# Row sums of causal attention over added pairs of exponentials: GpSimd adds, TensorE takes four steps in three groups

## The chip, the cores and the metric

The kernel runs on one core of a Trainium2 chip. The metric is the device time of one execution in microseconds (us), as the median of several runs. The core has five engines that work beside each other, each through its own queue in order: TensorE (PE, matrix products), VectorE (DVE), ScalarE (ACT), GpSimd (POOL) and SyncE (SP, which issues the transfers). PE writes its results to PSUM, eight banks of 128 x 512 float32; ACT and DVE read PSUM, POOL does not in this kernel.

## The reference, cut to what matters

One transformer block over 2048 tokens of width 512: a normalization, causal attention with 16 heads of 32, and a gated feed-forward part of width 4096, both added to the input. The change touches the attention alone:

```python
scores = jnp.einsum('bhqd,bhkd->bhqk', q, k) * scale
scores = jnp.where(causal, scores, jnp.finfo(scores.dtype).min)
probs = jax.nn.softmax(scores, axis=-1)
attn = jnp.einsum('bhqk,bhkd->bhqd', probs, v)
```

The softmax is not divided out before the product: the kernel sums `exp(score - max) * v` and `exp(score - max)` over the keys, and divides the one by the other at the end.

## The kernel before, in words

The work has four stages. Up to about 190 us tokens are normalized and transposed, values are made, and the queries, keys and row maxima of the first heads. From there to about 735 us runs the **main attention loop**, over six of the eight head pairs; then to about 848 us the **joint stage**, in which the last two pairs share each step; then the feed-forward part, which the change does not touch.

A head pair p has 40 steps, n = 0 to 39. A step is a block of 512 queries (qb) against a tile of 128 keys (kt). The query blocks come in the order 1, 2, 3, 0 with 8, 12, 16 and 4 steps: n = 0 to 7, 8 to 19, 20 to 35, 36 to 39. The last four steps of each block are on the diagonal, where only the last 512, 384, 256 and 128 columns are computed. They are the **diagonal** steps; all others are full.

The order on PE is written out by hand: the scheduler is off, and each engine gets its instructions in the order of the program. One step of the main loop (L508 to L533) issues, in this order:

- the transposes of finished maxima, if due (`rows_when_due`, L271), four steps after they were split up;
- `score_cols` (L290): for both heads, the product that puts minus the row maximum into a tile of the pool `ps_t`;
- `score_rows` (L216): scores with the queries in the partitions, for a later head pair, into two tiles of the pool `ps_s`. They serve only to find the row maxima;
- `add_scores` (L305): scores with the keys in the partitions, added to the `ps_t` tiles;
- `attend` (L358) for the step two before this one: a **group** of four products of 32 columns each, which lie side by side in the array's four column tiles: values of head 0, values of head 1, and for both heads a matrix of ones, which gives the row sums. All four go to one bank, `av`;
- `exponentials` on ACT (L319; on the diagonal L325, L327 and L329 and then `omit_later_keys`, L334, on POOL);
- `maxima` on DVE (L240, on the diagonal L235), and when a block's maxima are complete, `split` (L250 on DVE, L256 and L258 on POOL);
- `keep_attention`, if a query block was finished one step ago: ACT copies the values out of `av` (L378), DVE the sums (L379);
- `normalize_attention` (L391 on DVE, L393 on POOL), one quarter of a block per full step, after the second pair of each two;
- in some steps a projection of queries or keys for later heads (`project`, L172, eight passes, copied out by L184 or L186 on ACT).

PSUM is full: `ps_s` and `ps_t` have three banks each, and `ps_m` has two (m0 and m1). A step takes two tiles of `ps_s` and two of `ps_t`. The accumulators `av` take m0 and m1 in turn from one query block to the next, and the other one of the two is "spare": projections and transposed maxima use it. The exponentials of a step lie in one of four `prob` tiles.

Of the kernel before, what the change touches and what calls it, by code (L numbers as in the profile page):

```python
# [33 lines left out]
BF16 = mybir.dt.bfloat16  # L37
F32 = mybir.dt.float32
# [3 lines left out]
ALU = mybir.AluOpType  # L42
# [3 lines left out]
P = 128  # L46
# [3 lines left out]
D = H // HEADS  # L50
NT = S // P
TB = 512
NTB = S // TB
NK = H // P
NOG = H // P
NP = HEADS // 2
# [21 lines left out]
def block_kernel(  # L78
# [10 lines left out]
    nc = tc.nc  # L89
# [4 lines left out]
    def turn_tile(i, name, dtype=F32, shape=(P, TB)):  # L94
        return turns.tile(list(shape), dtype, tag=f"turn{i}", name=name)
# [17 lines left out]
    with (  # L113
# [24 lines left out]
        ones = const.tile([P, D], F32, tag="ones", name="ones")  # L138
        nc.vector.memset(ones, 1.0)

        turn = [0]
# [17 lines left out]

        qT, kT = {}, {}

        def project(og, b, which):
            for _ in project_halves(og, b, which):
                pass

        def project_halves(og, b, which):
            w = wqk[og]
            ps = spare(F32, f"ps_qk{og}_{b}_{which}")  # L170
# [21 lines left out]
        units, steps, first = [], [], {}  # L192
# [12 lines left out]
        def tile_of(pool, name):  # L205
            return pool.tile([P, TB], F32, tag="s" if pool is ps_s else "t", name=name)
# [52 lines left out]

            due.append((tick[0] + 4, p, qb, buf))  # L260

        def rows_from_parts(joint):

            _, p, qb, buf = due.pop(0)
            og, half = p // 2, slice(64 * (p % 2), 64 * (p % 2 + 1))
            if p < 2 or joint:
                pt = ps_t.tile([P, TB], BF16, tag="t", name=f"pm{p}_{qb}")
            else:
                pt = spare(BF16, f"pm{p}_{qb}")
# [6 lines left out]
        def rows_when_due(joint=False):  # L276
            if due and tick[0] >= due[0][0]:
                rows_from_parts(joint)
            tick[0] += 1

        def score_cols(p, n, pool):
# [59 lines left out]
                channel_multiplier=-1,  # L341
            )

        avs, sums = {}, {}

        def attend(p, n, prob, first=None, last=None):

            qb, kt = steps[n]
            if first is None:
                first, last = kt == 0, kt == 4 * qb + 3  # L350
            if first:
                turn[0] = (NTB * p + qb) % 2 if p < NP - 2 else p % 2
                avs[p, qb] = ps_m.tile([P, TB], F32, tag=f"m{turn[0]}", name=f"av{p}_{qb}")
            av = avs[p, qb]
            c0 = max(0, kt - 4 * qb) * P
            for h in range(4):
                head = 2 * p + h % 2
                nc.tensor.matmul(  # L358
                    av[D * h : D * (h + 1), c0:],
                    lhsT=v[kt // 4][:, kt % 4, D * head : D * (head + 1)] if h < 2 else ones,  # L360
                    rhs=prob[:, h % 2, c0:],
                    start=first,
                    stop=last,
                )
            if last:
                full.append((p, qb))

        full, invert = [], []

        def keep_attention():  # L370

            p, qb = full.pop(0)
            av = avs[p, qb]
            og, half = p // 2, slice(64 * (p % 2), 64 * (p % 2 + 1))
            if p % 2 == 0:
                sums[og, qb] = sump.tile([P, TB], F32, tag="sums", name=f"sums{og}_{qb}")
            if p < NP - 2:
                nc.scalar.copy(aT[og][qb][half], av[:64])  # L378
                nc.vector.tensor_copy(sums[og, qb][half], av[64:])  # L379
            else:  # L380
# [100 lines left out]
        for b in range(NTB):  # L481
            n = first[b]
# [24 lines left out]
        pending, waiting = [], False  # L507
        for m in range((NP - 2) * STEPS):  # L508
            p, n = divmod(m, STEPS)

            ahead = p + 3 if p % 2 == 0 else p + 1
# [12 lines left out]
            pending.append((p, n, prob))  # L524
            qb, kt = steps[n]
            if invert and kt < 4 * qb:
                normalize_attention()


            if own in places and og + 2 < NOG:  # L530
                project(og + 2, *places[own])
            if own in places_own and og > 0 and og + 1 < NOG:
                project(og + 1, *places_own[own])  # L533
# [40 lines left out]
        def token_rest(b, k, high):  # L574
# [8 lines left out]
            )  # L583
            yield

        early = [(i, k) for i in range(2) for k in range(NK)]
        rest = iter(())
        for s, n in enumerate(together):
            rows_when_due(joint=True)
# [3 lines left out]
            for _ in range(2):  # L593
# [405 lines left out]
```

## Time and profile before

| | us |
|---|---|
| median of 3 runs | 1992.45 |
| lowest, highest | 1990.56, 1992.8 |
| the profiled execution | 1993.41 |
| its span | 1991.7 |

| stretch of the profiled execution, us | length | PE busy | DVE busy | ACT busy | POOL busy |
|---|---|---|---|---|---|
| 205 to 735 (main loop) | 530 | 527.1 | 324.9 | 295.3 | 79.7 |
| 735 to 850 (joint stage) | 115 | 107.8 | 47.1 | 74.6 | 33.9 |
| 1000 to 1990 (feed-forward) | 990 | 985.9 | 712.6 | 604.4 | 521.5 |

The profile is of one execution. Its page gives the busy time of each engine, the span in 40 slices, the chain of work that ended last, and groups of instructions by line with count, mean duration in ns, and the idle time before them with what ended it. The timeline lists instructions in order of time: start, duration, engine, line, operation, what is written and read, the shape, the count, and in brackets the idle time ahead of it and its releaser. A stretch of the windows view has its length, busy time and count of PE, of PE's weight loads (PEld), DVE, ACT and POOL, then the granted clock of PE (1.00 is full), the share of the DMA engines and GB/s. A float32 product takes two passes, so a group of four products shows as eight.

### The profile page before, as it was taken

The page shows a single profiled execution, that of the slowest core. Times are in us where ns is not written, and L with a number is a line of the kernel's source. Part 1 is how long each engine was busy: PE and PEld are TensorE (multiplying, and loading weights), DVE is VectorE, ACT ScalarE, POOL GpSimd, SP SyncE. Part 2 cuts the span into 40 slices and gives each one's busy share as a digit, 9 for nine tenths or more (in the row PEclk, how much of TensorE's full clock was granted, in tenths as well). Part 3 has the DMA queues.
Part 4 walks back from the last instruction along what each step waited for, and adds up shares of the span by engine and source line. Part 5 has one row for each costly group of instructions (what it writes and reads, how often), then busy time and mean ns, then how long its engine had stood idle before and what let it go on. Part 6 is the DMA issues. An engine that isn't in the chain of part 4 may idle for free.

```text
span 1991.7 us, 31028 instructions
## 1 busy us (share of the span) xinstructions
PE 1958.1 (98%) x11072; PEld 1163.9 (58%) x11072; DVE 1326.4 (67%) x2706; ACT 1092.6 (55%) x2281; POOL 727.3 (37%) x893
## 2 busy tenths in 40 slices
PE   7999999999999999999999999999999999999998
PEld 3433233333333323246888888888888888888886
DVE  5657665646565665277777777777777777767674
ACT  2111664546455666634666666666666666666654
POOL 1000111201120224145555555555555555545451
PEclk9999999999999999999999999999999999999999
DMA  3000000000000000120000000000000000000002
GB/s 127 0 11 12 1 2 1 2 12 1 1 1 12 1 1 2 36 73 23 22 20 21 20 21 21 21 20 21 21 20 22 18 23 18 23 18 22 19 5 85
DMA packets 55387, 39.79 MB, mean 20 GB/s; under 512 B 14784, under 2 KB 47552, under 8 KB 55232
## 3 DMA queue, kind: packets, MB, share of 16 engines
q1 hardware_dynamic: 55232, 37.81, 6.4%
q8 instruction: 87, 1.43, 0.3%
q14 instruction: 68, 0.56, 0.1%
HBM read 33.55 MB, written 4.19 MB: 19 GB/s over the span
## 4 chain that ended last, share of the span: by engine, by line
PE 96%; ACT 2%; DVE 1%; issue 1%; DMA 0%; POOL 0%; DVEq 0%; SPq 0%; ACTq 0%; POOLq 0%
PE gu L851 24%; PE av L358 12%; PE gu L864 12%; PE pd L914 12%; PE ps_s L216 9%; PE ps_qk L172 6%; PE pd L926 6%; PE ps_t L290 4%; PE ps_t L305 3%; PE ps_v L462 3%; PE po L806 3%; ACT prob L319 1%; PE pm L271 1%; PE ptx L451 0%; ACT prob L566 0%
## 5 line engine op out<-in xcount | busy, mean ns | idle before, releaser
L851 PE MATMUL gu<-xh,gu 128*128 128x512 f32 x1024 | 404.3, 395 | 0.0
L851 PE MATMUL gu<-lm,gu 128*128 128x512 f32 x1024 | 404.2, 395 | 0.0
L240 DVE TENSOR_REDUCE tops<-ps_s 128x1 f32<-128x512 f32 x384 | 243.7, 682 | 159.0 <-PE ps_s L216 138.2
L935 DVE SCALAR_TENSOR_TENSOR acc<-pd,acc 128x512 f32<-128x512 f32 x512 | 317.0, 681 | 2.4 <-PE pd L926 2.4
L319 ACT ACTIVATE prob<-ps_t 128x512 f32<-128x512 f32 x384 | 205.9, 597 | 158.1 <-PE ps_t L305 156.7
L216 PE MATMUL ps_s<-qk,qk 32*128 32x512 f32 (+3 forms) x1280 | 292.0, 577 | 0.0
L358 PE MATMUL av<-prob,v 128*32 128x512 f32 (+3 forms) x1280 | 288.6, 540 | 2.0 <-issue 0.7
L358 PE MATMUL av<-prob,ones 128*32 128x512 f32 (+3 forms) x1280 | 288.5, 541 | 0.0
L864 PE MATMUL gu<-lm,gu 128*128 128x512 f32 x1024 | 279.8, 395 | 0.0
L896 POOL TENSOR_TENSOR parts<-inter,hi 128x512 fp32r<-128x512 f32 x128 | 171.2, 1338 | 278.2 <-DVE hi L892 273.0
L888 DVE SCALAR_TENSOR_TENSOR inter<-gu,gate 128x512 f32<-128x512 f32 x128 | 88.5, 691 | 275.3 <-PE gu L864 271.0
L305 PE MATMUL ps_t<-qk,qk 32*128 32x512 f32 (+3 forms) x1280 | 265.5, 537 | 0.0
L921 ACT ACTIVATE pd<-pd 128x512 f32<-128x512 f32 x512 | 263.4, 582 | 1.1 <-PE pd L914 1.1
L914 PE MATMUL pd<-wd,parts 128*128 128x512 f32 x1024 | 259.6, 396 | 0.0
L858 ACT ACTIVATE gu<-gu 128x512 f32<-128x512 f32 x256 | 148.7, 581 | 188.2 <-PE gu L851 188.1
L864 PEld LDWEIGHTS gu<-lm,gu 128*128 128x128 f32 x1024 | 192.3, 188 | 46.8 <-issue 0.2
L851 PEld LDWEIGHTS gu<-lm,gu 128*128 128x128 f32 x1024 | 192.2, 188 | 46.1 <-POOL wd L721 0.2
L914 PEld LDWEIGHTS pd<-wd,parts 128*128 128x128 f32 x1024 | 192.4, 188 | 45.6
L851 PEld LDWEIGHTS gu<-xh,gu 128*128 128x128 f32 x1024 | 192.2, 188 | 45.7 <-ACT wd L720 0.2
L334 POOL TENSOR_SCALAR_AFFINE_SELECT prob<-prob 128x256 f32<-128x256 f32 x128 | 52.2, 409 | 424.2 <-ACT prob L329 317.4
L235 DVE CUSTOM_DVE_ANT_0 ps_s<-ps_s,mask_qk 128x128 f32<-128x128 f32 (+3 forms) x256 | 120.8, 516 | 101.3 <-PE ps_t L305 55.7
L895 ACT CAST parts<-hi 128x512 fp32r<-128x512 f32 x128 | 79.7, 623 | 173.1 <-DVE hi L892 173.1
(98 smaller groups left out, 2672.1 us busy)
## 6 DMA issues: line engine op xcount, KB each, us to landing
pk<-packed SPq DMA_DIRECT2D x96, 128.0 KB, 2.2
sc<-scales SPq DMA_DIRECT2D x512, 8.0 KB, 1.6
x<-x SPq DMA_DIRECT2D x16, 256.0 KB, 3.9
acc<-x SPq DMA_DIRECT2D x16, 256.0 KB, 3.7
sc<-scales SPq DMA_DIRECT2D x256, 16.0 KB, 1.7
out<-acc SPq DMA_DIRECT2D x16, 256.0 KB, 2.2
wqk<-w_qk SPq DMA_DIRECT2D x4, 512.0 KB, 3.7
wv<-w_v SPq DMA_DIRECT2D x4, 256.0 KB, 6.5
```

Of the source, the lines that this page charges most:

```text
L216: nc.tensor.matmul(ps[:, :w], lhsT=qT[p // 2, qb][rows, i * P : (i + 1) * P], rhs=kT[p // 2, c][rows, :w], start=True, stop=True,)
L240: nc.vector.tensor_reduce(top, ps[:, :w], AX.X, ALU.max)
L305: nc.tensor.matmul(ps[:, c0:], lhsT=kT[p // 2, kt // 4][rows, (kt % 4) * P : (kt % 4 + 1) * P], rhs=qT[p // 2, qb][rows, c0:], start=False ...
L319: nc.scalar.activation(prob[:, h, :], ps, AF.Exp)
L358: nc.tensor.matmul(av[D * h : D * (h + 1), c0:], lhsT=v[kt // 4][:, kt % 4, D * head : D * (head + 1)] if h < 2 else ones, rhs=prob[:, h % ...
L851: nc.tensor.matmul(ps, lhsT=parts[:, i, k], rhs=mov, start=(k == 0 and i == 0), stop=(k == NK - 1 and i == 1),)
L858: nc.scalar.activation(ps, ps, AF.Copy, scale=HIGH_SCALE)
L864: nc.tensor.matmul(ps, lhsT=gu[g, m, j][:, 2, k], rhs=lm[b, k][1], start=False, stop=(k == NK - 1), skip_group_check=True,)
L896: nc.gpsimd.tensor_tensor(parts[:, 1], inter, high, ALU.subtract)
L914: nc.tensor.matmul(po, lhsT=parts[:, part, i * P : (i + 1) * P], rhs=w[:, part], start=(part == 0), stop=(part == 1),)
L921: nc.scalar.activation(po, po, AF.Copy, scale=HIGH_SCALE)
L935: nc.vector.scalar_tensor_tensor(acc[t], po, SUM_SCALE, acc[t], ALU.mult, ALU.add)
```

## The change

In the full steps of the main loop, the row sums are no longer taken for each step. POOL adds the exponentials of two neighbouring steps (two additions of 128 x 512, one for each head), and PE multiplies the added tile by the matrix of ones. Four full steps then need eight products with values and four with ones, which are put into three groups in place of four:

- `attend_pair`: the values of steps 0 and 1, each with both heads, in all four column tiles of `av`. Column tiles 2 and 3 of `av` so collect part of the values;
- `attend_with_rows`, twice: the values of step 2 (then 3) in column tiles 0 and 1 of `av`, and the ones over an added pair in column tiles 2 and 3 of another bank, `rows`.

The diagonal steps keep a group of their own, with values to `av` and sums to `rows`. `av` is now always m0 and `rows` always m1 in the main loop. So nothing is spare there: the projections take a tile of `ps_s`, the transposed maxima a tile of `ps_t`. `keep_attention` copies values and sums on ACT, and DVE adds the second half of the values (for query block 0, which has only diagonal steps, this is left out). It comes in the step in which the block's last group is issued, no longer one step later. The joint stage keeps groups of four products in one bank.

When a group is issued is set by `later_on`. The built order has, relative to the first step of four: the pair in step 3, the first group with sums in step 4, the second in step 6; a diagonal step's group comes three steps later, that of the last diagonal step two. So of a head pair's 40 steps, n = 2, 5, 10, 13, 17, 22, 25, 29, 33 and 38 issue no group, and n = 1, 9, 21 and 37 issue two (256 and 128 columns). Before, each step issued one.

The diff, cut to its core:

```diff
-        def spare(dtype, name):
-            i = (turn[0] + 1) % 2
-            return ps_m.tile([P, TB], dtype, tag=f"m{i}", name=name)
...
+        def add_values(p, n, prob, place, start, stop):
             qb, kt = steps[n]
             c0 = max(0, kt - 4 * qb) * P
-            for h in range(4):
-                head = 2 * p + h % 2
+            for h in range(2):
+                head = 2 * p + h
+                j = 2 * place + h
                 nc.tensor.matmul(
-                    av[D * h : D * (h + 1), c0:],
-                    lhsT=v[kt // 4][:, kt % 4, D * head : D * (head + 1)] if h < 2 else ones,
-                    rhs=prob[:, h % 2, c0:],
-                    start=first,
-                    stop=last,
-                )
+                    avs[p, qb][D * j : D * (j + 1), c0:],
+                    lhsT=v[kt // 4][:, kt % 4, D * head : D * (head + 1)],
+                    rhs=prob[:, h, c0:],
+                    start=start,
+                    stop=stop,
+                )
+
+        def add_rows(p, qb, probs, c0, start, stop):
+            for h in range(2):
+                nc.tensor.matmul(
+                    rows[p, qb][D * (2 + h) : D * (3 + h), c0:],
+                    lhsT=ones,
+                    rhs=probs[h][:, c0:],
+                    start=start,
+                    stop=stop,
+                )
+
+        def open_sums(p, qb):
+            avs[p, qb] = ps_m.tile([P, TB], F32, tag="m0", name=f"av{p}_{qb}")
+            rows[p, qb] = ps_m.tile([P, TB], F32, tag="m1", name=f"rows{p}_{qb}")
+
+        def attend_pair(p, n, prob_a, prob_b):
+            qb, kt = steps[n]
+            if kt == 0:
+                open_sums(p, qb)
+            add_values(p, n, prob_a, 0, kt == 0, False)
+            add_values(p, n + 1, prob_b, 1, kt == 0, kt == 4 * qb - 4)
+
+        def attend_with_rows(p, n, prob, added, start):
+            add_values(p, n, prob, 0, False, False)
+            add_rows(p, steps[n][0], added, 0, start, False)
...
+        def add_up(q, prob_a, prob_b):
+            added = []
+            for h in range(2):
+                t = turn_tile(2 * (q % 4) + h, f"added{q}_{h}")
+                nc.gpsimd.tensor_tensor(t, prob_a[:, h], prob_b[:, h], ALU.add)
+                added.append(t)
+            return added
...
-            if p < NP - 2:
-                nc.scalar.copy(aT[og][qb][half], av[:64])
-                nc.vector.tensor_copy(sums[og, qb][half], av[64:])
-            else:
-                copy = nc.scalar.copy if p % 2 == 0 else nc.vector.tensor_copy
-                copy(aT[og][qb][half], av[:64])
-                copy(sums[og, qb][half], av[64:])
+            copies = [nc.scalar.copy] * 2
+            if p == NP - 1:
+                copies = [nc.vector.tensor_copy] * 2
+            copies[0](aT[og][qb][half], av[:64])
+            if p < NP - 2 and qb > 0:
+                nc.vector.tensor_tensor(aT[og][qb][half], aT[og][qb][half], av[64:], ALU.add)
+            copies[1](sums[og, qb][half], row[64:])
...
-            if len(pending) == 2:
-                attend(*pending.pop(0))
+            run_due(m)
             prob = exponentials(p, n, ps)
             maxima(ahead, n, ps_max)
-            if waiting:
+            while full:
                 keep_attention()
-            waiting = bool(full)
-            pending.append((p, n, prob))
             qb, kt = steps[n]
+            if kt >= 4 * qb:
+                later_on(2 if kt == 4 * qb + 3 else 3, attend_diagonal, p, n, prob)
+            elif kt % 2 == 0:
+                even = prob
+            else:
+                added = add_up(2 * quads + kt % 4 // 2, even, prob)
+                if kt % 4 == 1:
+                    later_on(2, attend_pair, p, n - 1, even, prob)
+                    added_first = added
+                else:
+                    later_on(1, attend_with_rows, p, n - 1, even, added_first, kt == 3)
+                    later_on(3, attend_with_rows, p, n, prob, added, False)
+                    quads += 1
             if invert and kt < 4 * qb:
                 normalize_attention()
             if own in places and og + 2 < NOG:
-                project(og + 2, *places[own])
+                b, which = places[own]
+                project(og + 2, b, which, tile_of(ps_s, f"ps_qk{og + 2}_{b}_{which}"))
```

More of the change, by code (lines that the diff above doesn't have):

```diff
@@ L139, in block_kernel @@
         nc.vector.memset(ones, 1.0)
-        turn = [0]
-        def spare(dtype, name):
-            i = (turn[0] + 1) % 2
-            return ps_m.tile([P, TB], dtype, tag=f"m{i}", name=name)
         v = [vals.tile([P, 4, H], F32, tag=f"v{b}", name=f"v{b}") for b in range(NTB)]
@@ L162, in block_kernel, with project, project_halves @@
         qT, kT = {}, {}
-        def project(og, b, which):
-            for _ in project_halves(og, b, which):
+        def project(og, b, which, ps=None):
+            for _ in project_halves(og, b, which, ps):
                 pass
-        def project_halves(og, b, which):
+        def project_halves(og, b, which, ps=None):
             w = wqk[og]
-            ps = spare(F32, f"ps_qk{og}_{b}_{which}")
+            if ps is None:
+                ps = ps_m.tile([P, TB], F32, tag="m1", name=f"ps_qk{og}_{b}_{which}")
             for k in range(NK):
@@ L260, in split, with rows_from_parts @@
             due.append((tick[0] + 4, p, qb, buf))
-        def rows_from_parts(joint):
+        def rows_from_parts():
             _, p, qb, buf = due.pop(0)
             og, half = p // 2, slice(64 * (p % 2), 64 * (p % 2 + 1))
-            if p < 2 or joint:
-                pt = ps_t.tile([P, TB], BF16, tag="t", name=f"pm{p}_{qb}")
-            else:
-                pt = spare(BF16, f"pm{p}_{qb}")
+            pt = ps_t.tile([P, TB], BF16, tag="t", name=f"pm{p}_{qb}")
             for i in range(4):
@@ L274, in rows_from_parts, with rows_when_due @@
             nc.scalar.copy(negs[og, qb][half], pt[half])
-        def rows_when_due(joint=False):
+        def rows_when_due():
             if due and tick[0] >= due[0][0]:
-                rows_from_parts(joint)
+                rows_from_parts()
             tick[0] += 1
@@ L342, in omit_later_keys @@
             )
-        avs, sums = {}, {}
-        def attend(p, n, prob, first=None, last=None):
+        avs, rows, sums = {}, {}, {}
+        def add_values(p, n, prob, place, start, stop):
             qb, kt = steps[n]
-            if first is None:
-                first, last = kt == 0, kt == 4 * qb + 3
+            c0 = max(0, kt - 4 * qb) * P
+            for h in range(2):
[8 more added lines that the diff above has]
+                )
@@ new lines, in add_rows @@
+        def add_rows(p, qb, probs, c0, start, stop):
+            for h in range(2):
+                nc.tensor.matmul(
+                    rows[p, qb][D * (2 + h) : D * (3 + h), c0:],
[7 more added lines that the diff above has]
+            rows[p, qb] = ps_m.tile([P, TB], F32, tag="m1", name=f"rows{p}_{qb}")
@@ new lines, in attend_pair, with attend_diagonal @@
+        def attend_pair(p, n, prob_a, prob_b):
[7 more added lines that the diff above has]
+            add_rows(p, steps[n][0], added, 0, start, False)
+        def attend_diagonal(p, n, prob):
+            qb, kt = steps[n]
+            if kt == 0:
+                open_sums(p, qb)
+            last = kt == 4 * qb + 3
+            add_values(p, n, prob, 0, kt == 0, last)
+            add_rows(p, qb, [prob[:, h] for h in range(2)], (kt - 4 * qb) * P, kt == 0, last)
+            if last:
+                full.append((p, qb))
@@ L351, in attend @@
+        def add_up(q, prob_a, prob_b):
[5 more added lines that the diff above has]
+            return added
+        def attend(p, n, prob, first, last):
+            qb, kt = steps[n]
             if first:
-                turn[0] = (NTB * p + qb) % 2 if p < NP - 2 else p % 2
-                avs[p, qb] = ps_m.tile([P, TB], F32, tag=f"m{turn[0]}", name=f"av{p}_{qb}")
@@ L354, in attend @@
-            av = avs[p, qb]
+                avs[p, qb] = ps_m.tile([P, TB], F32, tag=f"m{p % 2}", name=f"av{p}_{qb}")
+                rows[p, qb] = avs[p, qb]
+            add_values(p, n, prob, 0, first, last)
             c0 = max(0, kt - 4 * qb) * P
-            for h in range(4):
-                head = 2 * p + h % 2
-                nc.tensor.matmul(
-                    av[D * h : D * (h + 1), c0:],
-                    lhsT=v[kt // 4][:, kt % 4, D * head : D * (head + 1)] if h < 2 else ones,
-                    rhs=prob[:, h % 2, c0:],
-                    start=first,
-                    stop=last,
-                )
+            add_rows(p, qb, [prob[:, h] for h in range(2)], c0, first, last)
@@ L372, in keep_attention @@
             p, qb = full.pop(0)
-            av = avs[p, qb]
+            av, row = avs[p, qb], rows[p, qb]
             og, half = p // 2, slice(64 * (p % 2), 64 * (p % 2 + 1))
@@ L376, in keep_attention @@
                 sums[og, qb] = sump.tile([P, TB], F32, tag="sums", name=f"sums{og}_{qb}")
-            if p < NP - 2:
-                nc.scalar.copy(aT[og][qb][half], av[:64])
-                nc.vector.tensor_copy(sums[og, qb][half], av[64:])
-            else:
-                copy = nc.scalar.copy if p % 2 == 0 else nc.vector.tensor_copy
-                copy(aT[og][qb][half], av[:64])
-                copy(sums[og, qb][half], av[64:])
+            copies = [nc.scalar.copy] * 2
[5 more added lines that the diff above has]
+            copies[1](sums[og, qb][half], row[64:])
             if p % 2 == 1:
@@ L506, in block_kernel, with later_on, run_due @@
         places_own = {5: (2, 1), 6: (2, 0), 14: (3, 1), 16: (3, 0), 26: (0, 0)}
-        pending, waiting = [], False
+        todo, at, quads = {}, [0], 0
+        def later_on(wait, f, *args):
+            todo.setdefault(at[0] + wait, []).append((f, args))
+        def run_due(m):
+            for f, args in todo.pop(m, []):
+                f(*args)
         for m in range((NP - 2) * STEPS):
             p, n = divmod(m, STEPS)
+            at[0] = m
             ahead = p + 3 if p % 2 == 0 else p + 1
@@ L530, in block_kernel @@
             if own in places and og + 2 < NOG:
-                project(og + 2, *places[own])
+                b, which = places[own]
+                project(og + 2, b, which, tile_of(ps_s, f"ps_qk{og + 2}_{b}_{which}"))
             if own in places_own and og > 0 and og + 1 < NOG:
-                project(og + 1, *places_own[own])
+                b, which = places_own[own]
+                project(og + 1, b, which, tile_of(ps_s, f"ps_qk{og + 1}_{b}_{which}"))
             if og + 2 < NOG and own == 20:
@@ L584, in token_rest @@
             yield
+        pending = []
         early = [(i, k) for i in range(2) for k in range(NK)]
@@ L588, in block_kernel @@
         for s, n in enumerate(together):
-            rows_when_due(joint=True)
+            rows_when_due()
             two = [score_cols(NP - 2, n, ps_t), score_cols(NP - 1, n, ps_s)]
@@ L592, in block_kernel @@
                 add_scores(NP - 2 + i, n, two[i])
-            for _ in range(2):
+            for m in sorted(todo):
+                run_due(m)
+            while pending:
                 attend(*pending.pop(0))
```

## The prediction, on record before the changed kernel ran

> **What bounds the kernel now.** I read the page first: engine shares, slices, the chain.
>
> ```profile
> PE 1958.1 (98%) x11072; PEld 1163.9 (58%) x11072; DVE 1326.4 (67%) x2706; ACT 1092.6 (55%) x2281; POOL 727.3 (37%) x893
> ...
> PEclk9999999999999999999999999999999999999999
> ...
> PE 96%; ACT 2%; DVE 1%; issue 1%; DMA 0%; POOL 0%; DVEq 0%; SPq 0%; ACTq 0%; POOLq 0%
> ```
>
> TensorE looks like the whole story: 98% busy, 96% of the chain. But the change touches only the attention loop (205 to 735 us), so I read that stage step by step in the timeline. Let T be the start of a step's value group (L358), which is when its scores are done; the gap is the time from T to the next step's first score matmul (L216).
>
> ```profile
> 507.14 0.30 PE L358 MATMUL av<-prob,v 128*32 128x128 f32 x2
> 507.14 1.29 DVE L240 TENSOR_REDUCE tops<-ps_s 128x1 f32<-128x512 f32 x2 [0.70 <-PE ps_t L305]
> ...
> 507.29 1.09 ACT L319 ACTIVATE prob<-ps_t 128x512 f32<-128x512 f32 x2 [0.87 <-PE ps_t L305]
> ...
> 507.50 0.81 PE L290 MATMUL ps_t<-neg,ones_h 3*128 3x512 bf16 x2
> ...
> 507.94 0.19 PEld L216 LDWEIGHTS ps_s<-qk,qk 32*128 32x128 f32 x2 [0.35 <-DVE tops L240]
> 507.94 0.70 PE L216 MATMUL ps_s<-qk,qk 32*128 32x512 f32 x2
> ...
> 509.10 0.62 PE L358 MATMUL av<-prob,v 128*32 128x512 f32 x2
> ...
> 510.10 0.70 PE L216 MATMUL ps_s<-qk,qk 32*128 32x512 f32 x2
> ...
> 510.35 0.58 ACT L378 COPY aT<-av 64x512 f32<-64x512 f32 x1
> ...
> 510.96 0.69 DVE L379 COPY sums<-av 64x512 f32<-64x512 f32 x1 [0.57 <-ACT aT L378]
> ...
> 511.27 0.62 PE L358 MATMUL av<-prob,v 128*32 128x512 f32 x2
> ...
> 511.69 0.95 DVE L391 RECIPROCAL sums<-sums 128x128 f32<-128x128 f32 x1
> ```
>
> Two things are to be seen. A 512-wide group has a gap of 0.99 us (509.10 to 510.09), and scores take 1.18, so a full step is 2.17. But the 128-wide group at 507.14 ends at 507.50 and the next scores start only at 507.94: a gap of 0.80, though the group needs 0.36. The score buffers are three per pool and a step takes two, so the second tile of the next step waits for the first exponential (507.29 + 0.60) and the first maximum (507.14 + 0.65). PE counts as busy there, because the first L290 already runs. So **the gap is the longer of the group and 0.80**. After a diagonal step with 384-wide scores I read 0.75 (359.85 to 360.60).
>
> **The change, part by part.** In the built order the matmuls of L358 fall from 1280 to 1136: 144, that is 36 groups (six per head pair, six pairs in the loop). At 0.99 each that is 35.6 us, if nothing else were late. Where do they go? Per head pair (40 steps, n = 0 to 39), steps n = 2, 5, 10, 13, 17, 22, 25, 29, 33, 38 have no group at all ("bare"), while n = 1, 9, 21, 37 get two (256 and 128 wide).
>
> 1. Bare, undisturbed: n = 13, 25, 29 fall from 0.99 to 0.80, 3 x -0.2 = -0.6; n = 5, 17, 33 follow a 384-wide step, 0.99 to 0.75, 3 x -0.25 = -0.75.
> 2. Doubled: 0.57 + 0.36 = 0.93 where the wait gave 0.79 (n = 37: 0.75): 3 x 0.14 + 0.18 = +0.6.
> 3. n = 7, 19, 35 and 39 now do the 512-wide diagonal group in place of the 384-wide one (0.79): 4 x 0.21, less 0.31 at n = 39, where the transposes (L271) waited for the DVE copy and now use another bank: +0.5.
> 4. n = 0, 8, 20, 36: the wait decides either way, 0.
>
> Together -0.25 per head pair.
>
> 5. Storing the sums (keep_attention) moves from the third step of a row block, which has a group, to the second, so that the next step is bare. ACT now copies twice (2 x 0.58) before the next exponentials, and DVE adds (0.69, taken from the L379 copy; the add has the same 64x512 output) after ACT's first copy. After T: exponentials to 1.25, copy to 1.83, add 1.86 to 2.55, next reduce to 3.24; the next T is at 0.93 + 1.18 = 2.11. The bare step's gap becomes 3.26 - 2.11 = 1.15, against 0.99: +0.16 at n = 10 and 22 of even pairs. In odd pairs a reciprocal (0.95) follows: the reduce ends at 4.2. The trace of before shows this same sequence (510.96, 511.69) but with a group and transposes over it and 0.69 us of stall left; T to the second next T is 5.38 either way; with the step behind it (gap 0.99 + 0.34 for the transposes, scores 1.18: 2.52) the new three steps take 7.90, where the old ones took 1.95 before the 5.38, 7.33. Of the 0.57, 0.14 is counted in 2: +0.41 at n = 10 and 22. At n = 38 the scores take only 0.43 to 0.65, so ACT's clip and exponential behind both copies, and DVE's masked maximum behind the add, give a gap of 1.6 against 1.0: +0.6. At n = 2 there is no add; -0.05. Even pairs: +0.88; odd pairs: +1.38.
> 6. Pairs 2 and 4: left-over reciprocals of the pair before lie under n = 9 to 12: +0.52; a stall of 0.69 at n = 4 goes, as the store ahead of it no longer uses DVE; at n = 5 a projection (3.6 us) stands behind the bare step and fills it, -0.75 more.
> 7. The first joint step gets three left-over groups instead of two: +0.8.
>
> Sum: pair 0: 0.63; pairs 1, 3, 5: 3 x 1.13 = 3.4; pairs 2 and 4: 2 x -0.29 = -0.6; joint 0.8: **+4.2 us**. Thus 35.6 us of PE work goes, and none of it is time.
>
> GpSimd's adds: 144 of the kind
>
> ```profile
> L896 POOL TENSOR_TENSOR parts<-inter,hi 128x512 fp32r<-128x512 f32 x128 | 171.2, 1338 | 278.2 <-DVE hi L892 273.0
> ...
> L722 POOL TENSOR_TENSOR gu<-gu 128x512 fp32r<-128x512 f32 x64 | 105.4, 1647 | 5.0
> ```
>
> and in the timeline of the feed-forward part
>
> ```profile
> 1202.78 1.36 POOL L896 TENSOR_TENSOR parts<-inter,hi 128x512 fp32r<-128x512 f32 x1 [0.80 <-DVE hi L892]
> 1202.89 2.48 DVE L935 SCALAR_TENSOR_TENSOR acc<-pd,acc 128x512 f32<-128x512 f32 x4
> ```
>
> 193 us at 1.34. A pair starts at its second exponential's end, T + 1.25, and ends at T + 3.9 (4.5 at 1.65); its first reader comes three steps on (the second pair's sums at L358's place), not before T + 5.5. Queued behind the adds on GpSimd are the zeroing of later keys (L334), read three steps later, the split of the maxima (four steps ahead of its transposes) and the normalizing products, which nothing in the loop reads. So 0, by either row; without this cover each 0.1 us over about 2.0 per add would be paid 144 times. The Trainium skill speaks against it ("Perfetto Trace Analysis", Optimizing Scalar/DVE Operations): GpSimd and VectorE share an SBUF read port, so moving work between them may not help. Held against 48 reciprocals of up to one add each that would be 64 us; but L935, with one input in SBUF as here, takes 0.62 each while L896 runs. I take 0, the nearest row; of the 64 the range takes in 15, since few reciprocals start under an add.
>
> **The clock** is the unknown. Where the loop starts, two steps have no group yet:
>
> ```profile
> 192.08 0.37 PE L290 MATMUL ps_t<-neg,ones_h 3*128 3x512 bf16 x1 [1.19 <-ACT prob L319]
> ...
> 193.97 0.37 PE L290 MATMUL ps_t<-neg,ones_h 3*128 3x512 bf16 x1 [0.54 <-ACT prob L319]
> ...
> 195.73 1.07 PE L358 MATMUL av<-prob,v 128*32 128x512 f32 x2
> ```
>
> and in two stretches of the windows view (length; busy time of PE, PEld, DVE, ACT, POOL; granted clock):
>
> ```profile
> 190.93:194.34 3.41, 1.72 (x15) 0.95 (x18) 2.05 (x4) 2.59 (x5) 0.22 (x1) 1.00 0.30 121
> 194.34:197.75 3.41, 3.41 (x21) 0.39 (x15) 1.48 (x3) 1.16 (x3) 0.00 (x0) 0.52 0.00 0
> ```
>
> After 3.41 us in which PE was busy for 1.72, the granted clock is 0.52 for the next 3.41 us, and a pass takes 1.07 instead of 0.62. The Trainium skill ("TensorE: Matmul & The Clock Gate", Why this matters for your kernels) asks only for no idle gap over about 3 us; by it the new waits cost nothing. The row says that gaps of 1.19 and 0.54 are enough. The measurement decides. At n = 10 and 22 of odd pairs and n = 10 of pairs 2 and 4 (eight places) PE idles some 1.5 us in the bare step: 1.9 busy of 3.41, near that row. At n = 38 it is about 1.1 idle. Bounds: none, and 14 places x 1.7 (half of 3.41) = 24 us. The row is near the threshold and the window's phase is chance, so I take half of the eight, at 1.2 each as part of the slow window lies over waits: **+4.8**.
>
> Sum: 4.2 + 4.8 = 9.0 on the profiled execution's 1993.41 (its span is 1991.7, with 1.7 around it), which gives 2002.4 and lies 1.0 above the median; on the median 1992.45 that is 2001.45, so **2001.5 us**.
>
> **Rivals.** (a) Not slower: the copies of step 5 don't delay the next scores, because ACT or DVE reach them earlier than I have it. Place: n = 2, 10, 22, 38. Point of decision: the first reduce behind the store ends within 0.80 after T. Then the 7.8 us of stores (0.88 + 3 x 1.38 + 2 x 1.40) go, these 24 bare steps save 0.2 each, and the clock stays: 4.2 - 7.8 - 4.8 = -8.4, 1984. For it: only that other gaps were read exactly; against: ACT and DVE run in order. Chance 0.15. (b) PE's 98% is real and the whole 35.6 us comes off: 1957. The 0.80 at 507.14 speaks against. 0.03. (c) As summed, clock untouched: 1996.7. 0.17. (d) GpSimd's adds take over 2.0 us, or block DVE: 15 us and more on top, 2016 and up. 0.15. (e) Forecast, 2001.5: 0.50. That the change does not do what it says is ruled out by the built order.
>
> **Numbers.** About 0.2% (4 us) is what a measurement of this kernel can tell from no change. Faster: (a) and (b), 0.18. Same: half of (c), 0.08 of (e): 0.16. Slower: 0.66. The range leaves out (b), the lower half of (a) and the far half of (d), 0.18 together: 1983 to 2017; it holds both ends of the clock's cost but for its last microseconds.
>
> **What would show it.** Right: L358's successors lose 144 matmuls, yet the loop lasts 530 us or more; gaps after bare steps of 0.75 to 0.80, and 1.1 to 2.1 behind a store; PE's share in the loop down to about 94%; adds near 1.34 us with no PE wait on them; some 3.4 us stretches at clock 0.5. Wrong: bare steps with gaps well under 0.75, or full groups over 1.0.

## The result and the profile after

| | before | after |
|---|---|---|
| median, us | 1992.22 (6 runs) | 2004.09 (6 runs) |
| lowest to highest | 1990.56 to 1992.8 | 2002.28 to 2007.1 |
| profiled execution, its span | 1993.41, 1991.7 | 2004.01, 2002.3 |

The ratio of after to before is 1.0062, with a 95% interval of 1.0049 to 1.0075: slower by 0.6%. The forecast was 2001.5.

The page of after, in the lines that answer to those of before:

```profile
PE 1931.5 (96%) x10784; PEld 1165.7 (58%) x10784; DVE 1323.6 (66%) x2700; ACT 1107.8 (55%) x2305; POOL 907.6 (45%) x1037
...
PEclk9999999999999999999999999999999999999999
...
PE 94%; ACT 4%; DVE 1%; issue 1%; DMA 0%; DVEq 0%; ACTq 0%
```

PE has 288 passes fewer (11072 to 10784: 144 float32 products of two passes), is busy for 26.6 us less, and the kernel takes longer. In the chain PE gave up two points and ACT gained two: some of what was work is now waiting for ACT.

The same stretch of the main loop as before, in the windows view:

```profile
205.00:735.00 530.00, 491.33 (x4002) 161.52 (x3996) 314.97 (x699) 299.55 (x746) 249.70 (x375) 0.98 0.01 3
```

PE is busy for 491.3 of 530 us (527.1 before), POOL for 249.7 (79.7 before). The granted clock is 0.98 where it was 1.00; over 530 us that small number is worth most of the loss, as the table and e1 below show.

To find where the time went I lined up the steps of both traces, each from its first score matmul to the next one's, and summed the differences. A stretch at half clock is 3.41 us in which PE is granted a clock of 0.50. On the two profiled spans (10.6 us apart):

| part | us |
|---|---|
| before the loop starts | -1.3 |
| loop, steps 2 and 3 of pair 0 | -1.9 |
| loop, all other steps, gaps alone | +2.4 |
| loop, seven stretches at half clock | +10.9 |
| joint stage and later, with an eighth stretch | +0.5 |

**A bare step**, n = 25 of pair 3, in the timeline of after:

```profile
517.70 0.62 PE L344 MATMUL av<-prob,v 128*32 128x512 f32 x2
...
518.71 0.70 PE L210 MATMUL ps_s<-qk,qk 32*128 32x512 f32 x2
...
519.79 0.37 PE L281 MATMUL ps_t<-neg,ones_h 3*128 3x512 bf16 x1
519.86 1.29 DVE L234 TENSOR_REDUCE tops<-ps_s 128x1 f32<-128x512 f32 x2
520.04 1.09 ACT L310 ACTIVATE prob<-ps_t 128x512 f32<-128x512 f32 x2 [1.09 <-PE ps_t L296]
520.69 0.37 PE L281 MATMUL ps_t<-neg,ones_h 3*128 3x512 bf16 x1 [0.53 <-ACT prob L310]
520.69 0.70 PE L210 MATMUL ps_s<-qk,qk 32*128 32x512 f32 x2
```

The group at 517.70 is followed by scores at 518.71. Behind those scores nothing is issued, and yet the next scores come only at 520.69: their `ps_t` tile is free when the first exponential of 520.04 is done. The step takes 1.98 us with no group in it, against 2.17 with one. That is the whole gain of a left-out group: 0.19 us and not 0.99.

**A doubled step and a store**, n = 21 to 24 of pair 3:

```profile
508.22 0.41 PE L344 MATMUL av<-prob,v 128*32 128x256 f32 x2
508.22 1.29 DVE L234 TENSOR_REDUCE tops<-ps_s 128x1 f32<-128x512 f32 x2 [0.70 <-PE ps_t L296]
...
508.67 0.28 PE L344 MATMUL av<-prob,v 128*32 128x128 f32 x2
...
509.02 0.70 PE L210 MATMUL ps_s<-qk,qk 32*128 32x512 f32 x2
...
509.49 0.58 ACT L423 COPY aT<-av 64x512 f32<-64x512 f32 x1
...
510.09 0.58 ACT L426 COPY sums<-rows 64x512 f32<-64x512 f32 x1
510.09 0.69 DVE L425 TENSOR_TENSOR aT<-aT,av 64x512 f32<-64x512 f32 x1 [0.59 <-ACT aT L423]
...
510.82 0.95 DVE L434 RECIPROCAL sums<-sums 128x128 f32<-128x128 f32 x1
511.34 0.37 PE L281 MATMUL ps_t<-neg,ones_h 3*128 3x512 bf16 x1 [0.87 <-ACT prob L310]
...
511.80 1.29 DVE L234 TENSOR_REDUCE tops<-ps_s 128x1 f32<-128x512 f32 x2
...
512.55 0.18 PEld L210 LDWEIGHTS ps_s<-qk,qk 32*128 32x128 f32 x1 [0.91 <-DVE tops L234]
...
513.12 1.06 PE L210 MATMUL ps_s<-qk,qk 32*128 32x512 f32 x1
```

From top to bottom: two groups (256 and 128 columns) start at 508.22, and the next scores at 509.02, 0.80 later: both fit into the wait. Then ACT copies twice, DVE adds and inverts, and the scores of the next step get their second tile only at 512.55, when the first maximum behind the reciprocal is done; 4.33 after the groups' start (the forecast had 4.2 for it). And at 513.12 one score pass of 512 columns takes 1.06 us, where 0.59 is usual.

The stretches of the windows view on both sides of that point:

```profile
509.61:513.02 3.41, 2.46 (x15) 0.69 (x10) 2.86 (x5) 2.12 (x4) 2.39 (x3) 1.00 0.00 0
513.02:516.44 3.42, 3.42 (x18) 0.54 (x12) 2.93 (x5) 1.09 (x2) 1.91 (x3) 0.50 0.00 0
```

After the waits of the store, PE gets half its clock for 3.41 us. In after's trace that happens eight times from 205 us on: at 267.26, 294.57, 513.02, 557.39, 591.53, 659.79, 710.99 and 745.13. (The last 1 to 3 us of the program, at half clock in every trace, are not counted.) Before, only the stretch at 194.34 was so; after lacks that one, which is the -1.9 of the table. In the loop a stretch makes its steps 1.4 to 1.6 us longer than the same steps elsewhere (step 23 of pair 3 takes 5.19, that of pair 1 3.61); the seven sum to 10.9.

All eight starts are whole multiples of 3.4133 us apart (27.31 is 8 of them, 245.76 is 72): cut into windows of that length from 267.26 on, the trace shows a granted clock of 0.50 for each of the eight and 1.00 for the window ahead of it. The Trainium skill ("TensorE: Matmul & The Clock Gate", What's actually happening) says that PE's activity is judged in windows of 3413 ns that run freely, without regard to the kernel, and the grid of the trace agrees. In this trace the phase of the windows also fits where a wait is paid for and where not: steps 11 and 23 of pair 1 stall alike, yet

```profile
291.15:294.57 3.42, 2.47 (x14) 0.69 (x16) 3.36 (x5) 1.46 (x3) 1.71 (x3) 1.00 0.00 0
294.57:297.98 3.41, 3.41 (x20) 1.15 (x22) 2.24 (x4) 1.66 (x3) 3.09 (x4) 0.50 0.00 0
318.46:321.87 3.41, 2.73 (x17) 0.76 (x16) 3.35 (x6) 1.38 (x3) 1.39 (x3) 1.00 0.02 5
321.87:325.28 3.41, 3.41 (x36) 1.23 (x32) 3.25 (x6) 2.41 (x5) 3.24 (x4) 1.00 0.00 0
```

the waits of step 11 (from 291.33 on) lie inside one window, and the next is at half clock; those of step 23 begin at 318.19, ahead of the edge at 318.46, and nothing follows. The wait behind the bare step 38 does the same. Behind pair 3 it is

```profile
553.98:557.39 3.41, 1.81 (x33) 0.94 (x29) 2.23 (x6) 3.10 (x12) 0.82 (x2) 1.00 0.00 0
557.39:560.81 3.42, 3.42 (x25) 1.34 (x26) 1.30 (x9) 1.42 (x6) 1.51 (x6) 0.50 0.00 0
```

and its 1.45 to 1.60 us of idle PE lie whole in one window behind pairs 0, 3, 4 and 5, which half clock follows each time, and across an edge behind pairs 1 and 2, where none follows. The phase is not the whole rule, though: in the trace of e6 the window from 738.99 holds the whole wait too, with PE busy for 1.81 of 3.41, and full clock follows.

The six runs of after show the clock from another side. They took 2002.3 us at a mean granted clock of 0.995, 2004.0 to 2004.2 at 0.993, and 2006.8 to 2007.1 at 0.991 to 0.992: the same program, faster or slower with its share of half clock.

### The profile page after: what moved, and what is told of

Same layout as the page of the kernel before. It is cut to its first block, busy times and chain, and to the rows that moved or that the text cites. A ratio compares the mean times of both kernels' runs of the same rounds, so it can differ in the third digit from the quotient of the medians.

```text
span 2002.3 us, 30630 instructions
## 1 busy us (share of the span) xinstructions
PE 1931.5 (96%) x10784; PEld 1165.7 (58%) x10784; DVE 1323.6 (66%) x2700; ACT 1107.8 (55%) x2305; POOL 907.6 (45%) x1037
## 4 chain that ended last, share of the span: by engine, by line
PE 94%; ACT 4%; DVE 1%; issue 1%; DMA 0%; DVEq 0%; ACTq 0%
PE gu L920 24%; PE gu L933 12%; PE pd L983 12%; PE av L344 11%; PE ps_s L210 9%; PE pd L995 6%; PE ps_qk L166 6%; PE ps_t L281 4%; PE ps_t L296 3%; PE ps_v L505 3%; PE po L875 3%; ACT prob L310 2%; PE pm L262 1%; PE ptx L494 0%; ACT prob L318 0%
## 5 line engine op out<-in xcount | busy, mean ns | idle before, releaser
L210 PE MATMUL ps_s<-qk,qk 32*128 32x512 f32 (+3 forms) x1280 | 298.0, 581 | 0.5
L965 POOL TENSOR_TENSOR parts<-inter,hi 128x512 fp32r<-128x512 f32 x128 | 171.5, 1340 | 277.9 <-DVE hi L961 272.7
L344 PE MATMUL av<-prob,v 128*32 128x512 f32 (+3 forms) x1280 | 252.0, 554 | 1.3 <-issue 0.7
L395 POOL TENSOR_TENSOR added<-prob,prob 128x512 f32<-128x512 f32 x144 | 180.0, 1272 | 143.3 <-ACT prob L310 142.8
L964 ACT CAST parts<-hi 128x512 fp32r<-128x512 f32 x128 | 79.7, 623 | 173.1 <-DVE hi L961 171.3
L281 PE MATMUL ps_t<-neg,ones_h 3*128 3x512 bf16 (+3 forms) x640 | 126.2, 353 | 47.6 <-ACT prob L310 28.3
```

Source lines behind the costliest of these rows:

```text
L210: nc.tensor.matmul(ps[:, :w], lhsT=qT[p // 2, qb][rows, i * P : (i + 1) * P], rhs=kT[p // 2, c][rows, :w], start=True, stop=True,)
L281: nc.tensor.matmul(ps[:, c0:], lhsT=ones_h[rows, :], rhs=negs[p // 2, qb][rows, c0:], start=True, stop=False,)
L344: nc.tensor.matmul(avs[p, qb][D * j : D * (j + 1), c0:], lhsT=v[kt // 4][:, kt % 4, D * head : D * (head + 1)], rhs=prob[:, h, c0:], start ...
L395: nc.gpsimd.tensor_tensor(t, prob_a[:, h], prob_b[:, h], ALU.add)
```

## The experiments

The theory after the result: PE work that goes is not time, since each step waits for its score tiles; the loss is the clock, set off by the waits behind the stores, at steps 10, 22 and 38. The rivals: GpSimd's additions slow DVE or ACT; the shared banks and pools cost; or the stores alone are the loss and the clock only goes along with it.

**e1_fill: the clock alone.** After, with PE kept busy in the waits by products that are overwritten at once:

```diff
+                for _ in range(fill if h == 0 else 0):
+                    nc.tensor.matmul(ps, lhsT=ident_h, rhs=warm_h, start=True, stop=True)
...
+            slow = p % 2 == 1 or p > 0 and n == 11
+            fill = {3: 2, 11: 6 if slow else 2, 23: 6 if p % 2 else 2, 39: 5}.get(n, 0)
```

> The changed kernel with 2 to 6 extra bf16 products of 128 x 512 ahead of the first L281 of the steps n = 3, 11, 23 and 39, whose results are overwritten by the product that follows; they fall into the wait behind a store. If the slow-clock stretches cost what the step table of after says (seven in the main loop at about 1.55 us, one more after it, some 12 us), they go and the time falls from 2004 to about 1993 (1990 to 1996), at granted clock 0.999. If the time is lost in the waits themselves and the clock only follows them, PE gets more work and nothing is gained: 2004 or more.

Measured: 1995.07, ratio to before 1.0005 (0.9997 to 1.0013): no difference left. The same place (steps 22 and 23 of pair 3) in its timeline and windows view:

```profile
509.31 1.47 PE L284 MATMUL ps_t<-warm_h,ident_h 128*128 128x512 bf16 x5
...
512.20 0.59 PE L212 MATMUL ps_s<-qk,qk 32*128 32x512 f32 x1
```

```profile
508.70:512.12 3.42, 3.37 (x20) 1.11 (x16) 2.84 (x4) 2.15 (x4) 2.42 (x3) 1.00 0.00 0
512.12:515.53 3.41, 3.41 (x32) 0.96 (x30) 3.25 (x6) 1.79 (x4) 2.38 (x3) 1.00 0.00 0
```

The store still holds the scores up, but the idle time is filled, the clock stays at 1.00 and the pass takes 0.59. Adding 98 products to PE made the kernel 9 us faster. Nothing from 205 to 735 us runs at half clock; two stretches are left outside the loop, at 193.78 and 777.46. The stores' waits remain: steps 22 and 23 of pair 1, which no stretch touched in after, take 5.92 us together in both. So the third rival, that the waits alone are the loss, is out. All gaps of the loop together, those of the stores among them, come to the 2.4 us of the table, and the clock is the rest.

**e3_before_adds: GpSimd alone.** Before, with the 144 additions of pairs, which nothing reads:

```diff
+            elif kt < 4 * qb:
+                for h in range(2):
+                    t = turn_tile(2 * (quads % 4) + h, f"added{p}_{n}_{h}")
+                    nc.gpsimd.tensor_tensor(t, even[:, h], prob[:, h], ALU.add)
```

> The kernel before with the 144 GpSimd additions put in, their results read by nobody. If GpSimd costs neither VectorE nor anybody else time, 1992 (within 2 us of before). If the additions hold a port that VectorE's instructions need, or the four tiles of exponentials come free late, 2000 and more, with longer L240 and L391.

Measured: 1992.82, ratio 1.0001 (0.9993 to 1.0009). The maxima in before:

```profile
L240 DVE TENSOR_REDUCE tops<-ps_s 128x1 f32<-128x512 f32 x384 | 243.7, 682 | 159.0 <-PE ps_s L216 138.2
```

and here, with the additions:

```profile
L240 DVE TENSOR_REDUCE tops<-ps_s 128x1 f32<-128x512 f32 x384 | 243.7, 682 | 157.4 <-PE ps_s L216 137.1
...
L531 POOL TENSOR_TENSOR added<-prob,prob 128x512 f32<-128x512 f32 x144 | 180.2, 1273 | 132.7 <-ACT prob L319 131.6
```

180 us of additions beside them leave the maxima at 682 ns each, what they take in before, and the 60 reciprocals from 190 to 850 us take 942 ns each in both. The first rival falls.

**e7_before_pools: the moved tiles alone.** Before, with projections in `ps_s` and transposed maxima in `ps_t`, as after has them:

```diff
-                pt = spare(BF16, f"pm{p}_{qb}")
+            pt = ps_t.tile([P, TB], BF16, tag="t", name=f"pm{p}_{qb}")
...
-                project(og + 2, *places[own])
+                project(og + 2, *places[own], tile_of(ps_s, f"ps_qk{og + 2}_{own}"))
```

> The kernel before with its projections in the pool of the score rows and its transposed maxima in the pool of the score columns, as the change has them. If these pools have room in those steps: 1992, but for about 0.3 us at each n = 39, where the transposes no longer wait for a DVE copy, 1990 to 1993. If the two displaced tiles hold up the scores: 1996 or more.

Measured: 1992.95, ratio 1.0001 (0.9992 to 1.001). In its trace step 39 gets 0.25 to 0.40 shorter and the step behind it as much longer; on balance the pools cost nothing.

**e8_four_groups: the banks without the packing.** After's banks, order of the store and store, but a group for each step, two steps back, as before. There is no second half of values here, so the addition takes the sums' bank in its place and the attention values are not the reference's.

```diff
-                nc.vector.tensor_tensor(aT[og][qb][half], aT[og][qb][half], av[64:], ALU.add)
+                nc.vector.tensor_tensor(aT[og][qb][half], aT[og][qb][half], row[64:], ALU.add)
...
+            later_on(2, attend_diagonal, p, n, prob)
```

> The changed kernel with a group in each step two steps back, values to one bank and sums to the other, no packing and no GpSimd additions; the store adds rows of the other bank in the place of the second half of the values, which is not made, so the values are wrong. If the packing gains nothing and only bare steps cost (idle PE, slow clock), this is near 1992. If the pair of banks that every query block shares is a cost of its own, which the bare step behind a store hides, the first group of a block waits for the store: +0.45 at n = 2, 10 and 22, +1.3 at n = 38, about 2.8 per head pair, 17 in all: about 2009, without slow stretches.

Measured: 2015.13, ratio 1.0114 (1.0098 to 1.0129). Step 10 takes 3.3 to 3.4 us (2.16 before), step 38 3.5 to 3.7 (1.65). Step 10 of pair 1:

```profile
298.19 0.58 ACT L427 COPY sums<-rows 64x512 f32<-64x512 f32 x1 [0.76 <-DVE aT L426]
...
298.82 1.05 PE L355 MATMUL rows<-prob,ones 128*32 128x512 f32 x4 [0.22 <-ACT sums L427]
```

With both banks in use by every query block, the first group of a block waits for the store of the block before, which the two alternating banks of before never did. In after, a bare step stands just there. So part of what the bare steps are is room for that wait. The direction was as the bank theory had it, the size was larger than I had worked out; the copy here also waits 0.76 for the addition, and both read the one bank `rows`; in after, where they read two banks, they run side by side (510.09). So e8 holds more than the shared banks, and how much of its 22 us is theirs alone is open.

**e2_old_store and e6_no_add: the store.** The first has ACT copy the values and DVE the sums, the second only leaves the addition out. In both the second half of the values is missing from the output.

```diff
+            elif p < NP - 2:
+                copies = [nc.scalar.copy, nc.vector.tensor_copy]
             copies[0](aT[og][qb][half], av[:64])
-            if p < NP - 2 and qb > 0:
-                nc.vector.tensor_tensor(aT[og][qb][half], aT[og][qb][half], av[64:], ALU.add)
```

> The changed kernel with the store of before: ACT copies the values, DVE the sums, and the addition of the second half of the values is left out, so that part of the values is missing from the output. If ACT's second copy and DVE's addition behind ACT's first are what delays the next scores: the gap at n = 38 falls from about 1.7 to 0.9, at n = 10 and 22 of odd pairs the two steps lose 0.5, of even pairs 0.3: some 8 us, and most slow-clock stretches go with the shorter waits, 6 to 10 us: 1986 to 1991. If the single pair of banks or the GpSimd additions make the loss, it stays at 2000 or more.

Measured: 1987.67, ratio 0.9974 (0.9963 to 0.9985).

> The changed kernel without DVE's addition of the second half of the values, which is so missing from the output; both copies stay on ACT. If the addition is what holds the next maximum, the gaps behind a store shrink by about its 0.69 us and the time comes near 1992. If ACT's second copy is as late as the addition (exponentials behind it start 2.42 us after T, the reciprocal waits for the same copy), little is gained: about 0.1 us at each store, 1 to 3 us in all, and the slow-clock stretches stay: 1999 to 2004.

Measured: 1999.98, ratio 1.0035 (1.0023 to 1.0047). Taking DVE's addition away brings 4 us, moving the second copy from ACT to DVE as well another 12. In e6 ACT is just as late as in after, here for step 22 of pair 1:

```profile
318.67 0.58 ACT L424 COPY sums<-rows 64x512 f32<-64x512 f32 x1
...
319.92 0.37 PE L281 MATMUL ps_t<-neg,ones_h 3*128 3x512 bf16 x1 [0.87 <-ACT prob L310]
```

the same 0.87 as at 511.34 in after, and six stretches at half clock remain in the loop. In e2 step 38 falls from 2.21 to 1.5 and 2.37 to 1.8, and one such stretch is left in the loop. So ACT's second copy alone is late enough to set off the clock. Whether DVE's addition alone would be was not run. The cheap store is the one that gives each engine one thing to do.

**e5_spread: no bare steps.** If a step can't be shorter than its wait, the three groups of four steps should be spread over the four: each step gets part of a group, cut by columns, and no step more than the wait allows.

```diff
-                    later_on(2, attend_pair, p, n - 1, even, prob)
+                    later_on(1, attend_pair, p, n - 1, even, prob, 0, 2 * P)
+                    later_on(2, attend_pair, p, n - 1, even, prob, 2 * P, TB)
...
-                    later_on(1, attend_with_rows, p, n - 1, even, added_first, kt == 3)
-                    later_on(3, attend_with_rows, p, n, prob, added, False)
+                    for w, c, d in ((2, 0, 3 * P), (3, 3 * P, TB)):
+                        later_on(w, attend_with_rows, p, n, prob, added, False, c, d)
```

The first group with sums is cut in the same way (128 and 384 columns, one and two steps on), and a block's first diagonal group too.

> The changed kernel with its three groups spread over four steps by columns: pieces of 384 columns, or 256 and 128, in each full step in place of three full groups and a bare step. If a gap is the longer of the group and 0.80 us, each full step then has a gap of about 0.80 in place of 0.99: 21 steps per head pair at -0.2, some 26 us less than the changed kernel without its slow stretches, about 1972 (1964 to 1982), faster than both. If smaller pieces cost more than their columns, or the floor is not the wait for the first exponential and maximum, 1995 or more.

Measured: 1970.90, ratio 0.9891 (0.9878 to 0.9905). Two steps of its timeline:

```profile
510.64 1.29 DVE L234 TENSOR_REDUCE tops<-ps_s 128x1 f32<-128x512 f32 x2 [4.29 <-PE ps_s L210]
510.66 0.73 PE L345 MATMUL av<-prob,v 128*32 128x256 f32 x10
...
511.48 0.70 PE L210 MATMUL ps_s<-qk,qk 32*128 32x512 f32 x2
...
512.63 0.52 PE L345 MATMUL av<-prob,v 128*32 128x384 f32 x2
```

The group parts that start at 510.66 are followed by scores at 511.48, 0.82 later: about the 0.80 of the wait. A full step that no store, transpose or projection disturbs now takes 1.95 to 1.99, where before had 2.18 for each and after 1.99 for one and 2.16 to 2.18 for three. That is the sharpest sign for the wait: the same products and the same store, the groups cut by columns and put in other places, and 33 us between the two orders, of which 10.9 are the clock's in the loop.

**e9_spread_store: e5 and a lighter store.** ACT copies both halves of the values, DVE the sums, and GpSimd adds the halves in SBUF.

```diff
+                second = turn_tile(8 + qb % 2, f"second{p}_{qb}")
+                nc.scalar.copy(second[half], av[64:])
+                nc.gpsimd.tensor_tensor(
+                    aT[og][qb][half], aT[og][qb][half], second[half], ALU.add
+                )
```

> The kernel with spread columns (1970.9) with another store: ACT copies both halves of the values, the second one to SBUF, DVE copies the sums without waiting for ACT, and GpSimd adds the halves. The maximum behind a store comes 0.6 us earlier where a reciprocal follows (eight places), a little where not, 0.15 at n = 38: 5 to 6 us less, about 1965 (1962 to 1968). If ACT's two copies set the end everywhere, or GpSimd's addition holds others up, 1970 or more.

Measured: 1976.22, ratio 0.9919 (0.9904 to 0.9934): 5 us slower than e5, a miss. Its timeline at step 11 of pair 1:

```profile
288.80 1.27 POOL L436 TENSOR_TENSOR aT<-aT,second 64x512 f32<-64x512 f32 x1 [3.66 <-ACT second L435]
...
290.15 2.49 POOL L401 TENSOR_TENSOR added<-prob,prob 128x512 f32<-128x512 f32 x2
...
292.69 0.41 PE L357 MATMUL rows<-added,ones 128*32 128x128 f32 x2 [0.79 <-POOL added L401]
```

Here L436 stands ahead of the two additions for the row sums in GpSimd's queue, they start only at 290.15, and TensorE waits for the second: this step takes 4.04 (3.53 in e5). The sums are read two steps after the additions, sooner than in after, so these have no 1.27 us to spare. Query block 0's sums, now copied by DVE, cost too: step 3 of pair 2 takes 3.38 (2.44).

**e10_spread_store_late: the addition behind.** As e9, with the halves added behind the additions of the same step, and block 0's sums copied by ACT.

```diff
+            while halves and (kt >= 4 * qb or kt % 2 == 1):
+                whole, second = halves.pop(0)
+                nc.gpsimd.tensor_tensor(whole, whole, second, ALU.add)
```

> e9_spread_store with GpSimd's addition of the two value halves issued behind the two additions for the row sums in the same step, and the copy of query block 0's sums back on ScalarE. If e9 missed because the half addition (1.27 us) stood ahead of those additions and so held up the row sums' group, then the time falls below e5_spread's 1970.9: -0.65 us at each of the eight late store steps, -0.15 at each step 39, about -1 at the start of the loop, so about 1963.5 us (1960 to 1967). If GpSimd has no room for the half addition in any place, or the store's copies by ScalarE set the end, it stays at 1970 us or more.

Measured: 1963.77 (1963.51 to 1964.17), ratio 0.9856 (0.9840 to 0.9873), faster than before by 28.7 us. The same place:

```profile
286.90 1.26 POOL L610 TENSOR_TENSOR aT<-aT,second 64x512 f32<-64x512 f32 x1
...
288.81 0.28 PE L357 MATMUL rows<-added,ones 128*32 128x128 f32 x2
```

TensorE no longer waits for `added`; the step takes 3.07. The total came as expected, its parts less so: the late places gave 0.32 to 0.46 each instead of 0.65. Steps 2 and 3 of pair 0 gave some 1.4, since no half-clock stretch falls on them in this trace; e9 has the same, so it is no merit of this order.

## Why the prediction was right, step by step

The mechanism held: 144 products went, on balance none of it became time, and the clock was touched. Three terms of the sum were mis-sized (the doubled groups, the joint stage and the clock) and a fourth was not in it. Their signs differ, so they nearly offset each other, and that is luck.

- **Steps 1, 3, 4 (bare, diagonal, waiting steps)**: right. Bare steps with n = 13, 25, 29 fell by 0.19, n = 5, 17, 33 by 0.27; with the projections of pairs 2 and 4 they sum to -9.7 in the loop, forecast -9.6. Step 3 came to +0.7 per head pair (forecast +0.5), as n = 39 gave nothing back (+0.02 to +0.06, forecast -0.10).
- **Step 2 (doubled groups)**: mis-sized. "0.57 + 0.36 = 0.93" added the gaps of two groups read alone, which is more than two groups in a row take (0.80 from 508.22 to 509.02), no longer than the wait: n = 1, 9 and 21 grew by 0.01, n = 37 by 0.05. In place of +3.6 for the loop it was +0.5.
- **Step 5 (store)**: right in size and place. Odd pairs: n = 10 to 12 and 22 to 24 each +0.55, n = 38 +0.72 (forecast +0.57, of which 0.14 stood in step 2, and +0.6). Even pairs: +0.11 where +0.16 stood, one step later than I had put it, and +0.57 at n = 38.
- **Step 6**: right in kind. The stall at n = 4 of pairs 2 and 4 went (-0.69, as forecast); the left-over reciprocals cost about 0.4 (0.52), and another 0.16 at n = 2 of these pairs, where nothing was forecast.
- All gaps of the loop together: +2.4, forecast 4.2 less 0.8 for the joint stage, 3.4.
- **Step 7 (joint stage)**: wrong in sign. In place of +0.8 the table has +0.5 with a stretch in it, which by the other seven is worth some 1.55: the gaps are about -1.1. e6, which is as after there but for the left-out addition and has no stretch, agrees: from its last step's scores to the end it takes 1255.9 us, before 1257.1. Part of it is a wait of before that after's trace does not have, the first value group of the joint stage for the sums' copy:

```profile
741.84 0.62 PE L358 MATMUL av<-prob,v 128*32 128x512 f32 x2 [0.68 <-DVE sums L379]
```

  Where the other half microsecond comes from, and what the third left-over group costs, stays open.
- **GpSimd at nothing**: right, by e3, at 1272 ns each in after (forecast 1340). The sharing of a port that the prediction held against it did not show in the maxima or the reciprocals of e3; rival (d) is out.
- **The clock, +4.8**: mis-sized. Of the eight odd and late places four were hit, as supposed, but at 1.6 each and not 1.2. And n = 38, to which I gave nothing with "about 1.1 idle", was hit behind four of the six pairs: its idle time is 1.45 to 1.60. The last of the four stretches runs in the joint stage. The seven in the loop at 1.55 are 10.9, and e1 shows that they are the loss: with none in the loop 1995.07.
- **Not in the sum**: the half-clock stretch at the start of the loop, 194.34 in before, is missing from after's trace (-1.9), and the loop starts 1.3 us earlier. In e1 and e5 a stretch at half clock is there at the loop's start, in e9 and e10 it is not; the phase of the windows may be why, which no run isolates. The loop's start lies between 188.1 and 189.6 us in the traces of all runs, so the 1.3 is likely what runs differ by and no work of the change.

Summed, against the forecast: gaps of the loop -1.0, clock +7.7 (eight stretches), start -3.2, gaps of the joint stage -1.9, together +1.6 on the profiled spans. The forecast was near because of these signs, not because each term was.

**The rivals.** (a) needed the stores to be early; e2 shows what that is worth, 1987.67, and that after's store isn't so. (b), all 35.6 us, fails at the first bare step; yet e5, with the same products cut by columns, is 22 us faster than before: much of the work is time once it is shared out. (c), the sum without the clock, gave 1996.7, and e1, which is near that case, measured 1995.07.

## What to carry to other kernels

Work taken off an engine that shows 98% busy saves time only as far as the next wait of that step: find the shortest gap that a step can have (here 0.80 us behind its scores) and spread what is left evenly under it, instead of leaving some steps empty. Put a store where each engine has one thing to do, and new work on an in-order engine behind what TensorE reads next. Where waits are gathered into one place, count what the clock does with them: waits of about a microsecond each cost more in clock here (10.9 us) than all changes of the gaps come to on balance (2.4).

## What the runs showed of the hardware beyond that

- Half clock followed windows in which the trace counts single idle times of 0.7 to 1.6 us (0.72 ahead of 589.07 and 0.87 ahead of 511.34; 1.60 ahead of the score tile at 744.65 is the longest in the windows ahead of the eight stretches). The rule that the prediction weighed, no gap over about 3 us, is too wide here.
- PE's busy time, as the trace counts it, does not tell which windows count: windows with 2.70 and 2.47 of 3.41 were followed by half clock, others with 2.48 and 2.24 were not, nor was one with 1.81 in e6. A matmul that waits for its tile half-way is counted as busy (at 511.34, a score group of 1.98 us), which may be why; it wasn't settled.
- Products that are overwritten at once hold the clock up: in e1 98 of them (bf16, 512 columns) in 24 places were worth 9 us.
